# One written order for TensorE, ScalarE and VectorE in the units of a state space layer

## The chip, the core and the metric

The kernel runs on one core of a Trainium2 chip, as one launch. The core has five engines with a queue each: TensorE (PE: matrix products and transposes), VectorE (DVE), ScalarE (ACT), GpSimd (POOL) and SyncE (SP, which issues most of the DMAs).[...] The metric is the device time of a launch in microseconds (us), and the kernel before stands at a median of 3936.15 us over three runs (3933.37 to 3936.95).

## The reference

The model is a decoder of four layers on 2048 tokens (16 sequences of 128) with 256 features; each layer has a self-mixing part, a cross attention and a feed-forward part. The change is in the self-mixing part of layer 2, a bidirectional state space layer. Per direction it computes:

```python
zxbcdt = x @ in_w.T                         # z: 512, xBC: 768, dt: 8 heads
dt = jax.nn.softplus(zxbcdt[..., D_INNER + CONV_CH:] + dt_bias)
conv = sum((xp[:, k:k + l, :] * conv_w[:, k] for k in range(D_CONV))) + conv_b
xBC = silu(conv)                            # -> xs (512), B (128), C (128)
L = jnp.exp(segsum(Adt))
Y_diag = jnp.einsum('bcln,bcsn,bhcls,bcshp->bclhp', Cc, Bc, L, X)
y = ssd(xh, dt, A, B, C) + xh * D[None, None, :, None]
y = rmsnorm(y * silu(z), gnorm_w)
return y @ out_w.T
```

`x` is normalised over its features first, and the outputs of the two directions go through a common output matrix and are added to the residual. A sequence is one chunk of 128, so only `Y_diag` is left of the scan.

## The kernel before, in words

The program is written with a layer that schedules: the text issues instructions in some order, and a scheduler sets each engine's final order by priorities and by its own estimates, except where an instruction is marked `keep_in_program_order`. Marked instructions keep the written order among themselves on their engine. In the kernel before only the products and transposes of this layer are marked (`pinned`, L253, and `pinned_transpose`, L258; the profile gives all of them line 255 or 258, so tiles tell them apart). ACT and DVE are ordered by the scheduler.

`l2_attn` works on four groups `g` of four sequences (512 tokens in a group) and two directions `f` and `b`: 8 units, `m` from 0 to 7, with `g, i = divmod(m, 2)`. Each unit has these steps:

- `channels`: six channel blocks `ch` (0 to 3 are xs, 4 is B, 5 is C). For each: a 128x512 product `xBC` on PE (L1191), the convolution's first tap with its bias on ACT (L1194), its other three taps on DVE (L1199, `scalar_tensor_tensor` on PSUM), and `Silu` in place on ACT (L1202).
- `gates`: four products `z` (L1209) and their Silu (L1210).
- `sums`: cumulative sums of the decays by four small products `cs`, then `left` and `cs` on DVE (L1219, L1221) and `right` on POOL (L1223).
- For each half `n` of the heads: `decays` (eight products `seg` into two double PSUM tiles, then two `Exp` on ACT that give `w`, L1253); `products` for n = 0 (`cb`, copied by ACT, L1263); `by_token` (eight transposes `xtok`, then `xd` on DVE with the factor dt, L1275); `weigh` (`w` times `cb` on DVE, L1285); `outputs` (products `y`, then on DVE the `D` term, L1304, and the gate, L1305).
- `squares` (ACT, L1311), `lengths` (products `ss`, a copy `ssb` on DVE, a transpose `sst`, `Sqrt` on ACT, reciprocal on DVE) and `project` (four times four products `proj`, each added to x with the row's factor on DVE, L1334).

The units overlap by the order of the text in the loop at L1386: while unit m goes through its two halves, unit m+1's channels (4, 5, 0 in the first half; 1, 2, 3 in the second) and gates and unit m-1's lengths and projection are written between them.

PSUM limits how far an engine may run ahead: `b1` has four buffers of 128x512, which every one of `xBC`, `z`, `cs`, `cb`, `xtok`, `y`, `ss`, `sst`, `proj` and `pw` takes in turn, and `b2` has two double buffers, taken by `seg`. A product waits until the last reader of its buffer's former tile is through. ACT has to load a table of functions when it changes between Exp, Silu, Sqrt and Ln; the loads are instructions of their own in its queue.

Ahead of the units stand the normalisation of the four groups (L1156 to L1177: statistics, `rstd`, `ss`, the scaling of `h`, eight transposes `tr` per group and their copies to `hT`), unit 0's channels and gates, the products `dt` over all groups and the softplus chain on DVE and ACT (L1343 to L1377), and 16 products `pw` that merge the two output matrices (L1383, L1384).

Of the kernel before, what the change touches and what calls it, by code (L numbers as in the profile page):

```python
# [16 lines left out]
P = 128  # L17
# [12 lines left out]
class Decoder:  # L30
# [1076 lines left out]
    def l2_attn(self):  # L1107
# [15 lines left out]
        with self.tc.tile_pool(name="l2a", bufs=1) as wk:  # L1123
# [32 lines left out]
            for g in range(NG):  # L1156
# [21 lines left out]
            def start(m):  # L1178
                return dict(
                    xs=wk.tile([P, 6, GT], F, tag="xs", name="xs", bufs=2), z=wk.tile([P, 4, GT], F, tag="z", name="z", bufs=2)  # L1180
                )

            def channels(m, u, chs):

                g, i = divmod(m, 2)
                d = dirs[i]
                cw, cbias = self.c(f"L2_{d}_conv_w"), self.c(f"L2_{d}_conv_b")
                for ch in chs:
                    ps = self.b1("xBC")
                    for k in range(2):  # L1190
                        self.pinned(ps, wx[d][:, k, ch * P : (ch + 1) * P], hTs[g][:, k, :], start=k == 0, stop=k == 1)  # L1191
                    x = u["xs"][:, ch, :]
                    w = lambda k: cw[:, ch * 4 + k : ch * 4 + k + 1]
                    nc.scalar.activation(x, ps, AF.Identity, scale=w(3), bias=cbias[:, ch : ch + 1])  # L1194
                    x3, p3 = (v.rearrange("p (t n) -> p t n", t=GB) for v in (x, ps))
                    for n in range(1, 4):
                        late, early = slice(n, P), slice(0, P - n)
                        dst, src = (late, early) if d == "f" else (early, late)
                        nc.vector.scalar_tensor_tensor(  # L1199
                            x3[:, :, dst], p3[:, :, src], w(3 - n), x3[:, :, dst], ALU.mult, ALU.add  # L1200
                        )
                    nc.scalar.activation(x, x, AF.Silu)  # L1202

            def gates(m, u):
                g, i = divmod(m, 2)
                for c in range(4):
                    ps = self.b1("z")
                    for k in range(2):
                        self.pinned(ps, wz[dirs[i]][:, k, S(c)], hTs[g][:, k, :], start=k == 0, stop=k == 1)  # L1209
                    nc.scalar.activation(u["z"][:, c, :], ps, AF.Silu)  # L1210

            def sums(m, u):

                g, i = divmod(m, 2)
                ps = self.b1("cs")[:, 0:P]
                for t in range(GB):
                    self.pinned(ps[R(t), :], da[:, i, g * GB + t, :], upto[dirs[i]], start=True, stop=True)
                left = wk.tile([P, P], F, tag="left", name="left", bufs=2)
                nc.vector.tensor_scalar(left, ps, kind[:, 1:2], kind[:, 0:1], ALU.mult, ALU.add)  # L1219
                cs = wk.tile([P, P], F, tag="cs", name="cs", bufs=2)  # L1220
                nc.vector.tensor_scalar(cs, ps, kind[:, 0:1], kind[:, 1:2], ALU.mult, ALU.add)  # L1221
                right = wk.tile([P, NH, P], F, tag="right", name="right", bufs=1)
                nc.gpsimd.tensor_tensor(  # L1223
                    right,
                    cs.unsqueeze(1).to_broadcast([P, NH, P]),
                    each.unsqueeze(2).to_broadcast([P, NH, P]),
                    ALU.mult,
                )
                u["left"], u["right"] = left, right

            def decays(m, u, n):

                tiles = [self.b2("seg").rearrange("p (t n) -> p t n", t=2) for _ in range(2)]
                for t in range(GB):
# [3 lines left out]
                        never[dirs[m % 2]].unsqueeze(1).to_broadcast([P, 4, P]),  # L1238
# [3 lines left out]
                for t in range(GB):  # L1242
                    self.pinned(
                        tiles[t // 2][:, t % 2, :],
                        u["left"][R(t), :],
                        u["right"][R(t), 4 * n : 4 * n + 4, :].rearrange("p h l -> p (h l)"),
                        start=False,
                        stop=True,
                    )
                ws = []  # L1250
                for ps in tiles:
                    w = wk.tile([P, 2, 4, P], F, tag="w", name="w", bufs=2)
                    nc.scalar.activation(w.rearrange("p t h l -> p t (h l)"), ps, AF.Exp)  # L1253
# [3 lines left out]
            def products(m, u):  # L1257

                ps = self.b1("cb")
                for t in range(GB):  # L1260
                    self.pinned(ps[:, S(t)], u["xs"][:, 4, S(t)], u["xs"][:, 5, S(t)], start=True, stop=True)
                cb = wk.tile([P, GB, P], F, tag="cbm", name="cbm", bufs=2)
                nc.scalar.copy(cb.rearrange("p t n -> p (t n)"), ps)  # L1263
                u["cb"] = cb

            def by_token(m, u, n):

                g, i = divmod(m, 2)
                xd = self.hp.tile([P, GB, 4, 64], F, tag="h", name="xd", bufs=2)
                for t0 in (0, 2):  # L1270
                    ps = self.b1("xtok").rearrange("p (t c n) -> p t c n", t=2, c=2)
                    for t in range(2):
                        for c in range(2):
                            self.pinned_transpose(ps[:, t, c, :], u["xs"][:, 2 * n + c, S(t0 + t)])
                    nc.vector.tensor_tensor(  # L1275
                        xd[:, t0 : t0 + 2],
                        ps.rearrange("p t c (h d) -> p t (c h) d", h=2),
                        dt[:, i, g * GB + t0 : g * GB + t0 + 2, 4 * n : 4 * n + 4].unsqueeze(3).to_broadcast([P, 2, 4, 64]),
                        ALU.mult,
                    )  # L1280
                return xd

            def weigh(u, ws):
                for i, w in enumerate(ws):
                    nc.vector.tensor_tensor(  # L1285
                        w, w, u["cb"][:, 2 * i : 2 * i + 2, :].unsqueeze(2).to_broadcast([P, 2, 4, P]), ALU.mult
                    )

            def outputs(m, u, n, ws, xd):

                D = self.c(f"L2_{dirs[m % 2]}_D")
                for c in range(2):
# [10 lines left out]
                    x, z = u["xs"][:, 2 * n + c, :], u["z"][:, 2 * n + c, :]  # L1303
                    nc.vector.scalar_tensor_tensor(x, x, D[:, 2 * n + c : 2 * n + c + 1], ps, ALU.mult, ALU.add)  # L1304
                    nc.vector.tensor_tensor(z, x, z, ALU.mult)  # L1305
# [3 lines left out]
            def squares(m, u):  # L1309
                for c in range(4):  # L1310
                    nc.scalar.activation(sq[:, c, :], u["z"][:, c, :], AF.Square)  # L1311

            def lengths(m, u):

                ps = self.b1("ss")[:, 0:P]
                for c in range(4):
                    for t in range(GB):
                        self.pinned(ps[R(t), :], self.ones[:, 0:32], sq[:, c, S(t)], start=c == 0, stop=c == 3)
                s = wk.tile([P, P], F, tag="ssb", name="ssb", bufs=1)
                nc.vector.tensor_copy(s, ps)  # L1320
                ps = self.b1("sst")[:, 0:P]
                self.pinned_transpose(ps, s)
                rs = self.small([P, GB], "yss")
                self.rsqrt(rs, ps.rearrange("p (t n) -> p t n", t=GB)[:, :, 0], 1.0 / 512)
                u["rs"] = rs

            def project(m, u):
                g, i = divmod(m, 2)
                for t in range(GB):
# [688 lines left out]
```

## Time and profile before

| | us |
|---|---|
| median of three runs | 3936.15 |
| the profiled execution: device time | 3932.67 |
| its span, first to last instruction | 3931.0 |
| PE busy | 3587.0 (91%) |
| DVE busy | 2106.7 (54%) |
| ACT busy | 1441.8 (37%) |
| POOL busy | 490.4 (12%) |
| mean granted TensorE clock | 0.938 of full |
| stretch of the state space layer in the span | about 1809 to 2197 |

A matrix product in fp32 shows as two records, and the ends of PE's records are modelled, so a busy PE is not PE at its peak; the distance between the starts of two groups tells more. A bracket behind a row of the timeline gives the idle time of that engine before it and what ended it. A wait for several semaphores is put down to the one that came last. "PEclk" is the share of the full clock that TensorE was granted.

### The profile page before, as it was taken

Reading aid. Unit: us, or ns where it says so; the run is one execution under the profiler, and the core shown is the slowest. Engines: PE = TensorE matmul, PEld = TensorE weight load, DVE = VectorE, ACT = ScalarE, POOL = GpSimd, SP = SyncE. Lnnn points to the kernel's source line nnn. Section 1 sums busy time; section 2 is a strip of 40 time slices with the busy share of each in tenths; the row PEclk is TensorE's granted clock in tenths of the full one; section 3 lists DMA queues with packets and bytes.
Section 4 is the critical chain, followed back from the end, with each engine's and each line's share of the span. In section 5 each row is a group of like instructions: output and inputs, shape, how many; then the busy total and the mean of one; then the engine's idle time right before and its main releaser. Section 6 shows DMA issues by size and latency. Waiting matters only on the chain.

```text
span 3931.0 us, 52987 instructions
## 1 busy us (share of the span) xinstructions
PE 3587.0 (91%) x22096; PEld 1919.0 (49%) x22096; DVE 2106.7 (54%) x4165; ACT 1441.8 (37%) x1893; POOL 490.4 (12%) x620
## 2 busy tenths in 40 slices
PE   7988999999998899967898995679999999999999
PEld 4655555555556566634455564442222222223665
DVE  5436344444544444465666445247777777772440
ACT  2334111111134322255655221112666666664221
POOL 5322000000013211152000200120000000001100
PEclk9977799999999999988999996887999999999989
DMA  3000000000110100000000000820000000000000
GB/s 91 9 1 5 9 17 20 20 21 18 35 34 2 35 1 1 20 25 13 1 1 11 2 1 31 284 75 0 1 1 1 1 6 12 17 1 13 1 8 17
DMA packets 73638, 84.65 MB, mean 22 GB/s; under 512 B 5587, under 2 KB 61206, under 8 KB 73142
## 3 DMA queue, kind: packets, MB, share of 16 engines
q1 hardware_dynamic: 65510, 71.04, 5.8%
q10 hardware_dynamic: 6352, 6.03, 0.5%
q0 software_dynamic: 1536, 4.20, 0.3%
q8 instruction: 174, 2.85, 0.3%
q14 instruction: 66, 0.54, 0.0%
HBM read 71.02 MB, written 10.22 MB: 21 GB/s over the span
## 4 chain that ended last, share of the span: by engine, by line
PE 81%; DVE 10%; POOL 3%; ACT 3%; issue 2%; DMA 1%; POOLq 0%; ACTq 0%; DVEq 0%
PE st L1728 9%; PE acc L1728 6%; PE down L166 6%; PE gate L166 6%; PE up L166 6%; PE proj L255 5%; PE smax L1728 4%; PE st L255 4%; PE qT L166 3%; PE o L255 2%; PE h L255 2%; PE rb L255 2%; DVE mx L1776 2%; PE v L886 1%; PE kT L886 1%
## 5 line engine op out<-in xcount | busy, mean ns | idle before, releaser
L1776 DVE TENSOR_REDUCE mx<-smax 128x1 f32<-128x512 f32 x1024 | 635.0, 683 | 178.2 <-PE smax L1728 178.2
L1831 ACT ACTIVATE e<-st 128x1024 f32<-128x1024 f32 x512 | 521.4, 1023 | 351.9 <-PE st L1728 332.5
L1728 PE MATMUL st<-qT,kT 32*128 32x512 f32 x2048 | 569.0, 646 | 3.4 <-ACT e L1831 3.4
L649 DVE SCALAR_TENSOR_TENSOR x<-down,w_all,x 128x256 f32<-128x256 f32 x512 | 212.2, 477 | 315.3 <-PE down L166 315.3
L638 ACT ACTIVATE gs<-gate,cols 128x512 f32<-128x512 f32 x132 | 90.7, 687 | 583.8 <-PE gate L166 583.7
L1728 PE MATMUL smax<-kb,qb 32*128 32x512 bf16 x1024 | 274.1, 395 | 7.7 <-DVE mx L1776 5.4
L1728 PE MATMUL acc<-e,v 128*32 128x512 f32 x2048 | 274.4, 608 | 0.2 <-ACT e L1831 0.2
L166 PE MATMUL gate<-hT,expert 128*128 128x512 f32 x528 | 250.0, 596 | 0.0
L166 PE MATMUL down<-expert,gs 128*128 128x256 f32 x1056 | 249.4, 379 | 0.5 <-DVE gs L639 0.5
L166 PE MATMUL up<-hT,expert 128*128 128x512 f32 x528 | 248.7, 593 | 0.0
L166 PEld LDWEIGHTS down<-expert,gs 128*128 128x128 f32 x1056 | 200.6, 190 | 84.0 <-DVE gs L639 31.7
L1728 PEld LDWEIGHTS st<-qT,kT 32*128 32x128 f32 x2048 | 153.4, 184 | 154.6 <-issue 117.1
L1728 PEld LDWEIGHTS <-qb 32*128 32x128 bf16 x1024 | 54.3, 93 | 290.4 <-issue 276.8
L166 PEld LDWEIGHTS gate<-hT,expert 128*128 128x128 f32 x528 | 100.7, 191 | 126.6 <-issue 126.3
L166 PEld LDWEIGHTS up<-hT,expert 128*128 128x128 f32 x528 | 100.8, 191 | 72.1 <-issue 65.4
L988 DVE TENSOR_TENSOR cT<-o,rb 128x512 f32<-128x512 f32 x64 | 44.3, 692 | 164.6 <-ACT rb L986 164.6
L1728 PEld LDWEIGHTS acc<-e,v 128*32 128x32 f32 x2048 | 40.4, 108 | 187.0 <-issue 185.9
L986 ACT COPY rb<-rb 128x512 f32<-128x512 f32 x64 | 37.5, 585 | 252.4 <-PE rb L255 252.4
L166 PE MATMUL qT<-hT,L_xattn_Wq 128*128 128x512 f32 x256 | 115.8, 606 | 8.2 <-issue 4.3
L183 PE MATMUL tr<-ident,h 128*128 128x128 f32 x352 | 63.4, 327 | 58.5 <-DVE h L205 33.5
L255 PE MATMUL o<-e,v 128*32 128x128 f32 (+1 forms) x2048 | 105.9, 281 | 11.8 <-DVE nm L292 11.8
L639 DVE SCALAR_TENSOR_TENSOR gs<-up,cols,gs 128x512 f32<-128x512 f32 x132 | 99.0, 751 | 24.4 <-PE up L166 8.1
(512 smaller groups left out, 5725.3 us busy)
## 6 DMA issues: line engine op xcount, KB each, us to landing
W<-in_L_ffn_W_dram SPq DMA_DIRECT2D x46, 512.0 KB, 4.4
expert<-in_L_ffn_Wg_dram SPq DMA_DIRECT2D x32, 128.0 KB, 2.1
expert<-in_L_ffn_Wu_dram SPq DMA_DIRECT2D x32, 128.0 KB, 2.2
expert<-in_L_ffn_Wd_dram SPq DMA_DIRECT2D x32, 128.0 KB, 2.4
hs<-zero SPq DMA_DIRECT2D x23, 128.0 KB, 1.9
ys<-yo ACTq DMA_DIRECT2D x23, 128.0 KB, 3.9
hb<-hs ACTq DMA_DIRECT2D x5, 512.0 KB, 3.9
x<-in_x_dram SPq DMA_DIRECT2D x4, 512.0 KB
```

Source lines behind the costliest of these rows:

```text
L166: self.nc.tensor.matmul(out, lhsT, rhs, start=i == 0, stop=i == n - 1 and bias is None)
L183: self.nc.tensor.transpose(ps[:, t * P : (t + 1) * P], src[:, t, k * P : (k + 1) * P], self.ident)
L255: self.tc.keep_in_program_order(self.nc.tensor.matmul(*a, **k))
L638: nc.scalar.activation(gs, pg, AF.Silu, bias=bg)
L639: nc.vector.scalar_tensor_tensor(gs, pu, bu, gs, ALU.add, ALU.mult)
L649: nc.vector.scalar_tensor_tensor(xt, pd[:, t, :], w_all[:, o : o + 1], xt, ALU.mult, ALU.add)
L886: nc.tensor.matmul(ps, l, r, start=True, stop=False)
L986: nc.scalar.copy(rb, ps)
L988: nc.vector.tensor_tensor(cT, po, rb, ALU.mult)
L1728: self.tc.keep_in_program_order(nc.tensor.matmul(*a, **k))
L1776: nc.vector.tensor_reduce(mx[:, kc, j : j + 1], ps, AX.X, ALU.max)
L1831: nc.scalar.activation(e[:, 2 * jj : 2 * jj + 2, :], ps, AF.Exp, scale=1.0 / 16.0)
```

## The change

Nothing of what is computed changes, and the products keep their shapes. It has three parts.

First, the steps are taken apart so that the text can place each engine's share on its own: `channel` and `silu` of one block, `gate` of one block, `weigh` and `gated` apart from `by_token` and `outputs`, `project` and `add` of one sequence, and `sums` and `length` as generators that stop between their parts. `squares` is done by halves.

Second, ACT's and DVE's instructions of the units are marked to keep their written order too (`act`, `copy`, `tt`, `ts`, `stt`), as PE's already were.

Third, the written order is new, in the loop and ahead of it. Unit 0's channels and gates follow group 0's normalisation, ahead of the other three groups'; `sums` of unit 0 stands ahead of `pw`.

```diff
-            for g in range(NG):
+            def tokens(g):
                 ...
+            pin = self.tc.keep_in_program_order
+            act = lambda *a, **k: pin(nc.scalar.activation(*a, **k))
+            copy = lambda *a: pin(nc.scalar.copy(*a))
+            tt = lambda *a: pin(nc.vector.tensor_tensor(*a))
+            ts = lambda *a: pin(nc.vector.tensor_scalar(*a))
+            stt = lambda *a: pin(nc.vector.scalar_tensor_tensor(*a))
...
+            def weigh(u, n, ws, tiles):
+                ...
+                by_cb(0)
+                by_dt(0)
+                by_dt(1)
+                by_cb(1)
+                return xd
...
+            def length(u):
+                ps = self.b1("ss")
+                for c in range(4):
+                    for t in range(GB):
+                        self.pinned(ps[R(t), 0:P], self.ones[:, 0:32], sq[:, c, S(t)], start=c == 0, stop=c == 3)
+                s = wk.tile([P, P], F, tag="ssb", name="ssb", bufs=1)
+                pin(nc.vector.tensor_copy(s, ps[:, 0:P]))
+                yield
+                self.pinned_transpose(ps[:, P : 2 * P], s)
+                u.rs = self.small([P, GB], "yss")
+                act(u.rs, ..., AF.Sqrt, bias=self.eps[:, 0:1], scale=1.0 / 512)
+                pin(nc.vector.reciprocal(u.rs, u.rs))
+                yield
...
-            us = {0: start(0)}
-            channels(0, us[0], (4, 5, 0, 1, 2, 3))
-            gates(0, us[0])
+            tokens(0)
+            u = Unit(0)
+            for ch in (4, 5, 0, 1, 2, 3):
+                channel(u, ch)
+                silu(u, ch)
+            for c in range(4):
+                gate(u, c)
+            for g in range(1, NG):
+                tokens(g)
...
+            for _ in sums(u):
+                pass
             (16 products pw)
-            sums(0, us[0])
             for m in range(M):
-                (two halves: decays, products, by_token, weigh, next unit's
-                 channels, outputs, last unit's lengths and project, gates)
+                after = Unit(m + 1) if m + 1 < M else None
+                ws = decays(u, 0)
+                if last:
+                    gated(last, 1, ys)
+                products(u)
+                xt = by_token(u, 0)
+                if last:
+                    squares(last, 1)
+                xd = weigh(u, 0, ws, xt)
+                if after:
+                    channel(after, 4)
+                    channel(after, 5)
+                if last:
+                    mean = length(last)
+                    next(mean)
+                    if after:
+                        channel(after, 0)
+                    po = [project(last, t) for t in range(2)]
+                    next(mean)
+                    for t in range(2):
+                        add(last, t, po[t])
+                elif after:
+                    channel(after, 0)
+                ys = outputs(u, 0, ws, xd)
+                gated(u, 0, ys)
+                if last:
+                    for t in range(2, GB):
+                        add(last, t, project(last, t))
+                    if not last.i:
+                        (bias added to this group's x on POOL)
+                squares(u, 0)
+
+                ws = decays(u, 1)
+                xt = by_token(u, 1)
+                if after:
+                    cs = sums(after)
+                    next(cs)
+                xd = weigh(u, 1, ws, xt)
+                if after:
+                    next(cs)
+                    channel(after, 1); gate(after, 0); silu(after, 4)
+                    channel(after, 2); gate(after, 1); silu(after, 5)
+                    channel(after, 3); silu(after, 0); gate(after, 2)
+                    silu(after, 1); silu(after, 2); gate(after, 3); silu(after, 3)
+                ys = outputs(u, 1, ws, xd)
+                last, u = u, after
+            gated(last, 1, ys); squares(last, 1)
+            po = [project(last, t) for t in range(2)]
+            mean = length(last)
+            next(mean); next(mean)
+            for t in range(GB):
+                add(last, t, po[t] if t < 2 else project(last, t))
```

## The prediction

> **What bounds the kernel now.** I began with the page: TensorE (PE) is busy 91% of the span, so the state space layer counts by what TensorE loses in it. The stretches of the layer, in the view of busy time by window (columns: window, its length, busy us and instructions of PE, weight loads, DVE, ACT, POOL, then the granted clock):
>
> ```profile
> 1809.00:1856.00 47.00, 35.55 (x136) 19.53 (x135) 29.94 (x65) 25.73 (x41) 0.48 (x3) 0.88 0.03 7
> 1856.00:1896.00 40.00, 34.65 (x160) 17.88 (x160) 25.31 (x36) 22.30 (x28) 3.79 (x2) 0.83 0.06 23
> 1896.00:2156.50 260.50, 232.90 (x1355) 134.14 (x1352) 169.57 (x281) 152.75 (x195) 18.43 (x9) 0.97 0.02 5
> 2156.50:2197.00 40.50, 32.44 (x243) 24.45 (x243) 24.39 (x45) 13.68 (x17) 2.39 (x2) 0.87 0.00 1
> ```
>
> They are the opening, unit 0, units 1 to 6 and unit 7 with the end: 388 us. Units 1 to 6 take 43.4 us each, with DVE at 65% and ACT at 59%: no engine is full, so it is waits that cost. One unit runs from the `seg` group at 2026.82 to the next at 2068.94; in its timeline these are the largest stalls of PE (start, us, engine, line; in brackets the idle time before and who ended it):
>
> ```profile
> 2033.37 3.70 PE L255 MATMUL xBC<-hT,L_b_wx 128*128 128x512 f32 x8 [0.76 <-ACT cbm L1263]
> ...
> 2040.55 1.08 PE L255 MATMUL ss<-squares,ones 128*32 128x128 f32 x32 [0.86 <-ACT xs L1202]
> ...
> 2043.87 0.33 PE L258 MATMUL sst<-ident,ssb 128*128 128x128 f32 x1 [2.24 <-DVE ssb L1320]
> ```
>
> Ends are modelled, so I count PE by starts of one group to the next: two `seg` groups of 2.04, `cb` 0.89, two `xtok` 0.88, six channels 1.71, four gates 1.72, two `y` groups 1.90, four `proj` 1.69, `ss`, `cs`, `sst` 1.35 together: 35.8 us at full clock. The unit took 42.1. The largest hole (2.24) is `sst`, behind a DVE queue full of convolutions.
>
> The clock is the second loss. After the holes of the opening it halves:
>
> ```profile
> 1858.00:1860.00 2.00, 1.18 (x8) 0.51 (x8) 0.00 (x0) 0.00 (x0) 0.77 (x1) 0.50 0.19 67
> 1860.00:1862.00 2.00, 2.00 (x13) 1.16 (x6) 0.00 (x0) 1.05 (x2) 0.00 (x0) 0.50 0.00 0
> 1862.00:1864.00 2.00, 2.00 (x12) 2.00 (x11) 0.19 (x1) 1.47 (x2) 0.00 (x0) 0.50 0.04 8
> 1864.00:1866.00 2.00, 2.00 (x7) 1.28 (x7) 1.84 (x3) 0.00 (x0) 0.00 (x0) 0.84 0.00 0
> 1866.00:1868.00 2.00, 2.00 (x6) 0.80 (x6) 2.00 (x3) 0.78 (x1) 0.00 (x0) 1.00 0.00 0
> ```
>
> PE is busy again from 1858.83, and the clock is back only by about 1865.3.
>
> **The change part by part.** The built program shows that DVE and ACT stand in the written order, and no engine's order changes outside this layer.
>
> *Units 1 to 6.* I laid one unit out by hand from those starts, each instruction at the later of its queue's turn and its inputs (plus 0.3 us from PE to ACT or DVE, 0.05 between the others, as the timeline shows), with four `b1` buffers. DVE, start to start: convolution step 0.65, `w` 1.2, `xd` 0.65, four gated steps 2.86, `proj` add 0.45. ACT: `Exp` pair 1.94, copy 0.5, channel 0.75, `Silu` 0.6, square 0.6, table load 1.28. From the start of `seg` (0):
>
> - First half. Exponentials 2.15 to 4.1, `cb` copy to 4.6; DVE `w`, `xd` twice, `w` to 8.3, then channels 4 and 5 to 10.3 and 12.3, `ssb` 12.6, channel 0 to 14.6. PE: `cb`, `xtok`, channels 4 and 5 to 7.24 without a wait, `ss` 8.1, channel 0 to 9.8. First `proj` needs channel 4's buffer: 10.4 (0.6 lost); second needs channel 5's: 12.4 (0.3); then `sst` at 14.1, no longer waiting for `ssb`. `y` needs channel 0's buffer and the root: 14.7 (0.5). Two `proj`, and the second half starts at 20.0.
> - Second half. The squares must end (19.4) and the Exp table load (20.7) before the exponentials at 22.15: just hidden. `w` to 24.35, so PE goes on with `cs` and channel 1; the gate at 25.0 finds its buffer. Channels and gates alternate to 35.25 with 0.1 us waits; `y` ends at 37.15.
>
> So 37.15, of which 1.4 is wait. The other edits of a unit cost nothing of their own: the instructions are the same in number, and `sst` now lies in `ss`'s tile, one `b1` tile fewer, but held from 7.2 to the root at 14.7, which is in the wait of `y`. In units 2, 4 and 6 the next layer's `rstd` stands in ACT's queue before the exponentials; it needs the last two adds and their statistics (22.0), so rstd ends 22.35, load 23.6, exponentials 1.45 late; `w` and `xd` follow and the first gate waits 1.5 us: 38.7. Sum 3 × 37.15 + 3 × 38.7 = 227.6; I add 0.25 a unit for latencies not seen: 229. Before: 260.4. Gain 31.
>
> [...] I expect full clock. The trace of before has a granted clock of 0.91 in several 20 us windows here; each dip is a few us at half rate and lies in the 43.4.
>
> *ACT's table loads.* A unit loses one Silu load (exp, sqrt, exp, silu are left: 4 instead of 5 or, with rstd, 7):
>
> ```profile
> L1253 ACT ACT_TABLE_LOAD x17 | 21.8, 1283 | 0.9 <-PE seg L255 0.6
> ...
> L1202 ACT ACT_TABLE_LOAD x15 | 19.2, 1283 | 11.1 <-DVE xs L1199 11.1
> ```
>
> By the built programs 50 in the layer become 36: 14 × 1.28 = 18 us of ACT, which hides beside PE, so nothing in the sum. The row is 1.28 us, and at 2029.61 the next exponential follows its load by 0.01 us. [...] I take the row.
>
> *The opening.* Channels and gates of unit 0 now follow the first 8 transposes on PE, at about 1811.8 instead of 1824.4. But each ACT `Silu` stands before the next channel's ACT step, so a channel is a serial chain: ACT 0.78, three DVE steps 2.05, Silu 0.62, in all 3.5 us against 1.71 on PE. ACT also changes table four times round group 3's rstd and ss. By hand: channel 4 is through at 20.3 (+1800), 5 at 24.5, then four of 3.5 to 38.5; the last gate needs channel 3's buffer (37.9), so PE has it done at 39.7. Behind it in PE's queue are 24 transposes; group 3's normalisation stands behind all convolutions on DVE (h 44.5, x 45.7), ACT scales to 47.4, transposes and copies to 48.4. `dt` starts at 1848.4; before it was 1843.7: 4.6 us later. No DMA moves: SP's queue has the same order. On POOL the four bias adds stand one place earlier; each (2.35 us) runs from 20.8 in a unit, and the next `right` is not due before 27.5.
>
> *The fill behind dt.* The 16 `pw` products used to run in the hole of the softplus chain:
>
> ```profile
> 1843.72 1.94 PE L255 MATMUL dt<-hT,wdt 128*32 128x512 f32 x16
> ...
> 1846.89 7.09 PE L166 MATMUL pw<-L_wbT,out_w 128*128 128x256 f32 x32
> ...
> 1855.57 0.43 PE L255 MATMUL cs<-tri_up,da 128*32 128x128 f32 x8 [1.59 <-DVE da L1377]
> ...
> 1858.83 2.09 PE L255 MATMUL seg<-right,left 32*128 32x512 f32 x8 [1.86 <-POOL right L1223]
> ```
>
> Now `cs` stands before `pw`. From dt to cs takes 11.0 (11.8, less 0.8 of DVE steps that pw's evictions had delayed); then cs 0.4, pw 6.75, seg 2.04. The hole of 8 us halves the clock. [...] The trace shows some 6 us (1858.83 to 1865.3), so 3.0 lost. Dt to `cb` is then 23.2[...] against 17.1. With the later dt, `cb` comes 10.7 late.
>
> *Unit 0* has no proj or ss. Laid out likewise 33.2 us from `cb` to `cb`; its squares hold back the second exponentials until 17.6. Before: 37.2, with half a clock at both ends. Gain 4.0; unit 1 starts 6.7 late.
>
> *Unit 7 and the end*: 40.3 from seg to the last proj before. By hand 33.7, plus 2 for a clock halved by a 3.9 us wait for `w`: 35.8. Gain 4.5.
>
> Sum: +6.7 - 31.3 - 4.5 = -29. The profiled execution had a span of 3931.0 in 3932.7 us; it becomes 3902 and 3904. The median of the runs is 3.5 above it: 3936.15 - 29 = 3907. Bounds: latencies 0 to 1.5 us a unit more or less (9), opening 0 to 14 late instead of 10.7, end ±3.
>
> **The rivals.**
> - The full gain: units at PE's floor, 6 × 35.8 = 215, gain 46, and the opening no worse than before: with 4 and 4.5, 3882. For it: PE is the fullest engine. Against: the serial channels. 12 in 100.
> - Half the gain: DVE's strict queue puts 41 us on a unit, as its steps' own records (conv 0.74, w 1.26) are longer than their starts apart, and every proj waits. Gain 14, less 6.7, plus 4.5: 3924. 16 in 100.
> - Slower: in the ACT queue the squares of the first half stand before the exponentials of the second. If the gated product is late, exponentials, `w`, `xd` and the gates' buffers all slip and the PE clock halves. My slack there is 0.1 us, so every us late is a us of the unit; from 4.8 us a unit the change loses (29 / 6), and at 7 it gives 3949. For it: squares in before waited up to 8.2 us for DVE's z. Against: z is due at 18.7, and 3 us would already take another fault upstream. 7 in 100.
> - No effect, gains and opening cancelling: 3936. 4 in 100.
> - The forecast: 61 in 100.
>
> **How the numbers follow.** A measurement of this kernel can tell 0.2% (8 us) from no change. The forecast's own range is 3894 to 3920. Below lies the full gain; above, half the gain mostly. From 3887 to 3927 leaves out about 2 in 10. Faster (below 3928): forecast 0.61, full gain 0.12, most of half the gain 0.15, so 0.88. Within: 0.04 and 0.01 of half the gain. Slower (above 3944): 0.07.
>
> **What would show it.** Unit starts 37.4 us apart (39.0 with rstd); `sst` without a wait; a clock of 1.0 throughout units 1 to 6; `dt` near 1848, `pw` after `cs` at half clock; 36 table loads. Wrong if unit starts stay over 41 us apart, or exponentials of the second half start over 2 us after their seg.

## The result, and the profile after

The changed kernel takes 3909.95 us (median of five runs, 3909.65 to 3916.67), the kernel before 3936.15 (3927.30 to 3938.74). The ratio is 0.9941, 95% interval 0.9927 to 0.9956: 0.6% faster. The forecast was 3907.

Total times are a coarse ruler here. In the thirteen profiled executions of this study the layer's first transposes behind the last `down` start between 1803.80 and 1813.64 us, although every edit lies inside the layer. So I compare the layer by itself: from the transposes `tr` behind the last `down` of the layer ahead to the first `kT` of the cross attention that follows. Before: 1809.49 to 2196.60, 387.1 us. After: 1807.21 to 2174.28, 367.1 us. The layer gained 20.0 us; of the profiled execution's gain (3932.67 to 3909.95, 22.7) the other 2.7 lie outside it.

Busy time by stretch in the changed kernel (stretch, its length, busy us and instructions of PE, weight loads, DVE, ACT, POOL, then granted clock, DMA share and GB/s):

```profile
1807.00:1858.00 51.00, 31.96 (x94) 13.48 (x93) 28.01 (x57) 28.46 (x43) 0.48 (x3) 0.80 0.02 3
1858.00:1902.60 44.60, 40.52 (x201) 23.08 (x202) 28.84 (x44) 17.55 (x25) 3.79 (x2) 0.91 0.08 25
1902.60:2138.90 236.30, 226.32 (x1353) 129.91 (x1352) 175.65 (x280) 133.57 (x184) 18.44 (x9) 1.00 0.02 5
2138.90:2174.30 35.40, 30.50 (x243) 22.93 (x243) 21.68 (x40) 12.82 (x17) 2.35 (x1) 0.90 0.00 1
```

The third line is units 1 to 6: 236.3 us where they took 260.5, PE busy for 96% of it, and the clock at 1.00 instead of 0.97. The first two, opening and unit 0, got longer: `dt` starts 38.1 us after the first transposes (34.2 before), `cb` of unit 0 at 62.3 (51.4), unit 1 at 95.3 (86.6).

| | forecast | measured |
|---|---|---|
| `dt` of the opening | 4.6 later | 3.9 later |
| `dt` to `cb` | 23.2 | 24.2 |
| unit 1's start | 6.7 later | 8.8 later |
| units 1 to 6 | 229 (37.4 and 39.0 a unit, in turn) | 236.2 (39.37 every unit) |
| unit 7 and the end | 35.8 | 35.4 |
| the layer | 29 shorter | 20.0 shorter |

The same unit's timeline of PE as shown of before, now from 2020.67 (start, us, engine, line):

```profile
2024.58 3.60 PE L255 MATMUL xBC<-hT,L_b_wx 128*128 128x512 f32 x8
2028.11 1.08 PE L255 MATMUL ss<-squares,ones 128*32 128x128 f32 x32
...
2035.18 0.27 PE L258 MATMUL ss<-ident,ssb 128*128 128x128 f32 x1
...
2047.65 1.98 PE L255 MATMUL z<-hT,L_b_wz 128*128 128x512 f32 x4 [1.02 <-DVE xd L1185]
```

The three waits shown of before (0.76, 0.86, 2.24 us) carry no bracket any more. The largest wait left in the first half is 0.33 us. One new wait of a microsecond stands in the second half: the first gate, behind `xd`. The chain of the next unit's second half, whose `seg` starts at 2080.78, says where that comes from (the chain counts a group from where the one before it ends; the parts of a unit that are compared with the forecast below are measured by it):

```profile
2080.78 2.00 PE seg L255 x12
2082.78 0.01 issue
2082.79 0.08 ACT L1183
2082.87 1.21 issue
2084.09 1.03 ACT w L1183
2085.12 0.02 issue
2085.14 1.22 DVE w L1185
2086.36 0.61 DVE xd L1185
2086.98 0.04 issue
2087.02 1.98 PE z L255 x4
```

An ACT instruction without a tile name (0.08, then 1.21 counted as issue) stands between `seg` and the exponentials. ACT's own timeline names it:

```profile
2082.79 1.28 ACT L1183 ACT_TABLE_LOAD   x1 [2.97 <-PE seg L255]
2084.09 1.94 ACT L1183 ACTIVATE w<-seg 128x1024 f32<-128x1024 f32 x2
```

ACT was free for 2.97 us and loaded the Exp table only when `seg` was done. The layer holds 36 table loads, as forecast; here one of them is open in full.

The opening. Behind `dt` PE stands for 7.41 us, and then works at half clock (granted clock 0.50 from 1853 to 1862):

```profile
1845.30 3.95 PE L255 MATMUL dt<-hT,wdt 128*32 128x512 f32 x16
1849.93 0.66 PE L258 MATMUL dtt<-ident,dT 128*128 128x128 f32 x4 [0.68 <-ACT dT L1387]
1858.00 0.66 PE L255 MATMUL cs<-tri_up,da 128*32 128x128 f32 x8 [7.41 <-DVE da L1416]
1858.58 9.02 PE L166 MATMUL pw<-L_wbT,out_w 128*128 128x256 f32 x32
```

`pw` takes 9.02 us where it took 7.09, and `dt` itself 3.95 where it took 1.94 (granted clock 0.50 from 1846 to 1848; 1.00 under the `dt` of before).

### The profile page after: what moved, and what is told of

The parts are those of the page before. It is cut to its first block, busy times and chain, and to the rows that moved or that the text cites. A ratio compares the mean times of both kernels' runs of the same rounds, so it can differ in the third digit from the quotient of the medians.

```text
span 3908.2 us, 52952 instructions
## 1 busy us (share of the span) xinstructions
PE 3579.1 (92%) x22096; PEld 1911.3 (49%) x22096; DVE 2112.2 (54%) x4165; ACT 1419.5 (36%) x1879; POOL 490.8 (13%) x620
## 3 DMA queue, kind: packets, MB, share of 16 engines
q8 instruction: 174, 2.85, 0.3%
## 4 chain that ended last, share of the span: by engine, by line
PE 80%; DVE 10%; ACT 3%; POOL 3%; issue 2%; DMA 1%; SPq 0%; POOLq 0%; ACTq 0%; DVEq 0%
PE st L1805 9%; PE acc L1805 6%; PE down L166 6%; PE gate L166 6%; PE up L166 6%; PE proj L255 5%; PE smax L1805 4%; PE st L255 4%; PE qT L166 3%; PE o L255 2%; PE h L255 2%; PE rb L255 2%; DVE mx L1853 2%; PE v L886 1%; PE kT L886 1%
## 5 line engine op out<-in xcount | busy, mean ns | idle before, releaser
L1187 DVE SCALAR_TENSOR_TENSOR xs<-xBC,cols,xs 128x508 f32<-128x508 f32 x144 | 106.1, 741 | 22.2 <-ACT xs L1183 18.8
```

Source lines behind the costliest of these rows:

```text
L1187: stt = lambda *a: pin(nc.vector.scalar_tensor_tensor(*a))
```

## The experiments

My theory after the result: the units gained what the forecast says less one open table load and some tenths, and the opening lost in two separate places, the chain of Silus and the clock behind `dt`. The rival: the gain is ACT's and DVE's fixed order as such, or one cause lies behind both losses of the opening. Each run below is a variant of the changed kernel unless it says otherwise, and the layer's length is what is compared (changed kernel 367.1).

**A table load brought forward.** A one-element exponential behind the squares makes ACT load the table while it has nothing to do.

```diff
                 squares(u, 0)
+                act(pre, self.eps[:, 0:1], AF.Exp)
 
                 ws = decays(u, 1)
```

> A one-element Exp on ACT behind the first half's squares, so that the Exp table is loaded before the second half's exponentials are due. Theory (the load of 1.28 us waits for seg together with the exponential and so lies open in each unit): units 38.1 us apart instead of 39.37, the layer from the transposes behind the last down product to the first kT 358 us instead of 367.2. Rival (the exponentials are late because squares and rstd stand before them in ACT's queue): 39.4, as the new instruction stands behind the same squares.

Measured: 3909.59 us, layer 366.5. Units 1, 3 and 5 take 38.09 us, but units 2 and 4 now take 40.0 and unit 6 takes 42.0. ACT's timeline of unit 4 of this run:

```profile
2035.67 1.28 ACT L1183 ACT_TABLE_LOAD   x1
2036.96 0.20 ACT L1183 ACTIVATE pre<-eps 128x1 f32<-128x1 f32 x1
2037.18 1.28 ACT L191 ACT_TABLE_LOAD   x1
2038.48 0.30 ACT L191 ACTIVATE rstd<-bnmv,eps 128x4 f32<-128x4 f32 x1
2038.80 1.28 ACT L1183 ACT_TABLE_LOAD   x1
2040.09 1.94 ACT L1183 ACTIVATE w<-seg 128x1024 f32<-128x1024 f32 x2
```

The next layer's `rstd`, which nothing holds in place, fell between the early exponential and the real ones: a Sqrt table and a second Exp table in a row. In unit 6 PE stood 1.96 us ahead of the first gate, 1.64 in units 2 and 4, and there that gate took 3.47 us where it took 1.98 in units 2 and 4. The gain of the odd units was given back in the even ones. So the early exponential was left out there:

```diff
                 squares(u, 0)
+                if not (last and last.i):
+                    act(pre, self.eps[:, 0:1], AF.Exp)
```

> The one-element exponential of the run before is now left out in the units whose ACT queue also holds the next layer's rstd (2, 4 and 6), where it only added two table loads. Theory (the Exp table load stands with seg's wait and is open by its own 1.28 us in the second half of every unit without rstd): units 1, 3 and 5 take 38.1 us, 2, 4 and 6 stay at 39.4; also unit 0 and unit 7 gain up to 1.3 each; the layer from its first transposes to kT takes 367.2 - 3 x 1.28 - 0 to 2.6 = 361 to 363. Rival (the load is not what is open; the 38.1 of the run before came from something else the early instruction moved): units 1, 3 and 5 stay at 39.4, layer 367.

Measured: layer 362.9 (3916.18 us, with the layer beginning at 1813.64). Unit starts at 1909.17, 1947.27, 1986.64, 2024.74, 2064.11, 2102.21, 2141.59: 38.10 and 39.37 in turn. The layer gained 4.2: three times 1.28, and 0.4 in the other stretches. In each odd unit just the load's duration disappears, so it was the load that was open.

Why does it wait for `seg` at all? The built program's ACT queue in the second half of such a unit says (the run with the early exponential below the changed kernel):

```
changed kernel, unit 1:     Activation squares    waits DVE
                            LoadActFuncSet        waits PE
                            Activation w<-seg     waits Activation
with the early exponential: LoadActFuncSet
                            Activation pre<-eps
                            Activation w<-seg     waits PE, Activation
```

In this build the exponential has two semaphores to wait for, and the first of the two sits on the load right ahead of it. The kernel before has exponentials with one wait in units 1 to 6, and the loads ahead of them do not wait (in unit 1 the load starts at 1915.02, 1.03 us of waiting for `seg` follow it, and the exponentials start at 1917.33). The other two traces agree: in the changed kernel the load starts at 2082.79, when `seg` ends; with the early exponential, in unit 5, it starts at 2083.82, straight behind the squares, and the exponentials only at 2086.81, behind `seg`.

**The sums behind `pw`.** The first unit's `sums` moved behind the 16 `pw` products, where the kernel before had them.

```diff
-            for _ in sums(u):
-                pass
-
             pw = wk.tile([P, 2, 4, DM], F, tag="pw", name="pw")
...
+            for _ in sums(u):
+                pass
             M = 2 * NG
```

> Only unit 0's cumulative sums are put back behind the 16 pw products. Theory (pw lay in the hole of the softplus chain, and now stands open behind it): from dt to cb 17 us instead of 24.2, the layer 361 us instead of 367.2. Rival (the hole halves the clock anyway, and the seg group then pays it): 20 us, the layer 364.

Measured: 3905.00 us, layer 360.3, 6.8 shorter. PE's timeline:

```profile
1843.34 4.00 PE L255 MATMUL dt<-hT,wdt 128*32 128x512 f32 x16
1848.51 7.09 PE L166 MATMUL pw<-L_wbT,out_w 128*128 128x256 f32 x32
1857.18 0.42 PE L255 MATMUL cs<-tri_up,da 128*32 128x128 f32 x8 [1.59 <-DVE da L1416]
1860.44 2.09 PE L255 MATMUL seg<-right,left 32*128 32x512 f32 x8 [1.86 <-POOL right L1233]
1862.46 1.84 PE L255 MATMUL cb<-xs 128*128 128x128 f32 x8
```

`pw` at 7.09 fills the hole again and `dt` to `cb` is 19.1 in place of 24.2; another 1.7 came in unit 0. (It is not the expected 17 because `dt` still takes 4.00 where it took 1.94 before; at half clock in the changed kernel it took 3.95.) Two short waits are left (1.59, 1.86), and the clock halves once more there (0.50 from 1861 to 1863, `seg` 2.09), only later.

**Each Silu one channel later** in unit 0:

```diff
+            prev = None
             for ch in (4, 5, 0, 1, 2, 3):
                 channel(u, ch)
-                silu(u, ch)
+                if prev is not None:
+                    silu(u, prev)
+                prev = ch
+            silu(u, prev)
```

> In unit 0 each Silu stands one channel later in the text, so that ACT takes the next channel's first tap before it waits for this channel's convolution. Theory (ACT step, convolution and Silu in series make 3.72 us a channel): about 2.3 us a channel, dt 31 us after the transposes behind the last down product instead of 38.1, the layer 361 us. Rival (the table loads for group 3's roots and the 24 transposes behind the gates set it): dt at 36 or later, the layer 365 or more.

Measured: 3912.29 us, but the layer began at 1813.05; it takes 360.1, 6.9 shorter, with `dt` 30.5 after the first transposes. In the changed kernel ACT waits in every channel for the convolution, Silu to Silu 3.72 us:

```profile
1825.65 0.63 ACT L1183 ACTIVATE xs<-xs 128x512 f32<-128x512 f32 x1 [2.42 <-DVE xs L1187]
1826.18 0.76 ACT L1183 ACTIVATE xs<-xBC,cols 128x512 f32<-128x512 f32 x1
1829.37 0.63 ACT L1183 ACTIVATE xs<-xs 128x512 f32<-128x512 f32 x1 [2.43 <-DVE xs L1187]
```

The chain of the forecast was there, and one place in ACT's queue removes it.

**All rows ahead of the first unit's channels**, the order of before for this part:

```diff
-            tokens(0)
+            for g in range(NG):
+                tokens(g)
             u = Unit(0)
...
-            for g in range(1, NG):
-                tokens(g)
```

> All four groups are normalised before unit 0's channels, as before; all else as in the changed kernel. Theory (the series of Silu and channel costs, not the place): the chain starts 13 us later and nothing follows it, dt at 41 instead of 38.1, the layer 370 us. Rival (the place ahead of the other rows made dt late): dt at 34 as before, the layer 363.

Measured: 3916.64 us, layer 370.4; `dt` 43.2 after the first transposes instead of 38.1. With the serial chain in place, starting it early is worth 3.3 us of the layer.

**Nothing held on ACT and DVE.** The new text and PE's order stay; ACT and DVE are the scheduler's again (the planner of the expectation).

```diff
-            pin = self.tc.keep_in_program_order
+            pin = lambda i: i
```

> The changed kernel with its written order kept only on PE; on ACT and DVE the order is chosen by the planner again, as in the kernel before. In the built program the planner swaps only neighbours there: the order inside the pairs xd and w, Silu and the next channel, and the squares of unit 0 between its two exponentials. Theory (the new sequence of groups, above all on PE, and not the pinning of ACT and DVE is what gained): units of 39 to 41 us, opening up to 7 us shorter because Silus move behind the next channel's first step, layer 355 to 372. Rival (the pins on ACT and DVE are what gained): units back at 43.4 us and more, layer over 387.

Measured: 3899.05 us, layer 354.7, 12.4 shorter than the changed kernel. Units take 39.74 us, 0.37 longer. `dt` starts at 29.6 (38.1), unit 0 takes 30.4 from `seg` to `seg` (35.1). So in this run holding ACT and DVE to the text gains 2 us in units 1 to 6 and costs 14.5 ahead of them, and what the units gained over the kernel before comes for the most part (3.7 of 4.0 us a unit) from the new sequence of groups. In this build the exponentials of the second half carry one wait and the second half takes 17.4 us (18.7 in the changed kernel); the first half, in which a unit has five table loads where the changed kernel has one, takes 22.3 (20.7). That the loads cost this time is not shown.

**The order of before, held.** The kernel before, with ACT and DVE held to its own text (every `nc.scalar` and `nc.vector` call of the units):

```diff
+            pin = self.tc.keep_in_program_order
+            pinned_scalar_activation = lambda *a, **k: pin(nc.scalar.activation(*a, **k))
...
-                    nc.scalar.activation(x, x, AF.Silu)
+                    pinned_scalar_activation(x, x, AF.Silu)
```

> The kernel before, with its own sequence of groups and with the opening as before, but ACT and DVE held to the order in which its text names the operations. Theory (pins gain nothing by themselves; in that text each Silu stands right behind its channel's three steps and three channels follow one another in a half, a chain of 3.7 us a channel): units of 44 to 50 us, layer 392 to 440, slower than before. Rival (being held to a written order is itself the gain, because the planner's order was bad): units under 42 us, layer under 380.

Measured: 4003.56 us, layer 456.9: further out than I expected, units of 52.3 to 54.4 us. ACT in one of them:

```profile
2026.62 0.63 ACT L1179 ACTIVATE xs<-xs 128x512 f32<-128x512 f32 x1
2027.15 0.76 ACT L1179 ACTIVATE xs<-xBC,cols 128x512 f32<-128x512 f32 x1
2030.34 0.63 ACT L1179 ACTIVATE xs<-xs 128x512 f32<-128x512 f32 x1 [2.42 <-DVE xs L1183]
```

It is the opening's chain of 3.72 us a channel, now three times in every half. A fixed order is worth what the text puts into it; by itself it is no gain.

**The transpose of the lengths back in its old place**, straight behind `ss`:

```diff
                     next(mean)
+                    next(mean)
                     if after:
                         channel(after, 0)
                     po = [project(last, t) for t in range(2)]
-                    next(mean)
```

> The changed kernel with the transpose of the squared lengths put back to its old place, straight behind ss on PE: ahead of channel 0 and of the first two proj instead of behind them. Theory (on DVE ssb stands behind the six steps of channels 4 and 5, so it is done 12.7 us after the unit's start while PE reaches the transpose at about 8.5; PE waits some 4 us, partly given back because the first proj needs channel 4's buffer until 10.5 anyway): 2 to 4.5 us on a unit, units of 41.4 to 43.9, the layer at 381 to 394. Rival (the transpose's place costs nothing, the units' gain comes from the other orders): units stay at 39.4, layer 367.

Measured: 3942.68 us, layer 400.7, units of 44.2 to 45.0: more than either expectation. PE's timeline:

```profile
2042.65 1.08 PE L255 MATMUL ss<-squares,ones 128*32 128x128 f32 x32
2048.03 0.33 PE L258 MATMUL ss<-ident,ssb 128*128 128x128 f32 x1 [4.30 <-DVE ssb L1347]
2048.20 3.00 PE L255 MATMUL xBC<-hT,L_b_wx 128*128 128x512 f32 x4
2050.98 4.24 PE L255 MATMUL proj<-pw,z 128*128 128x256 f32 x16
```

PE waits 4.30 us for `ssb`, and channel 0, which started straight behind `ss` in the changed kernel (2029.12, 1.01 us after it), stands behind the transpose in PE's queue and waits with it. Then the clock is at half for 3.4 us (2048.8 to 2052.2, granted clock 0.50 in 2049 to 2052): channel 0 takes 3.00 instead of 1.98. The hole and its clock together cost 4.8 to 5.6 us a unit. With the other orders as they are, this one place in PE's queue is worth more than the units' whole gain over the kernel before (4.0 us a unit). Whether moving the transpose alone would have gained anything in the kernel before, where it waits 2.24 us, was not run.

**Taps of channels 4 and 5 in turn** on DVE:

```diff
-                    channel(after, 4)
-                    channel(after, 5)
+                    pair(after, 4, 5)
...
```

> The changed kernel, with the three steps of channels 4 and 5 of the next unit alternating on DVE (first tap of 4, first of 5, second of 4 ...) in place of one channel after the other. Theory (a convolution step that follows a step on the same tile starts 0.74 us behind it, one that follows a step on another tile 0.65): the six steps take 3.9 us in place of 4.4; channel 4's buffer comes free 1.5 us later, the first proj of the last unit with it, so a unit gains or loses at most 0.5 us. Rival (the 0.74 us is the step's own duration whatever precedes it): six steps 4.4 us still, and a unit about 1 us longer for the later buffer.

Measured: 3910.08 us, layer 365.4. Six steps in the changed kernel, in this run, and in the kernel before:

```profile
2028.73 4.50 DVE L1187 SCALAR_TENSOR_TENSOR xs<-xBC,cols,xs 128x508 f32<-128x508 f32 x6
```

```profile
1990.00 3.98 DVE L1187 SCALAR_TENSOR_TENSOR xs<-xBC,cols,xs 128x508 f32<-128x508 f32 x6
```

```profile
2051.99 3.99 DVE L1199 SCALAR_TENSOR_TENSOR xs<-xBC,cols,xs 128x508 f32<-128x508 f32 x6 [0.20 <-ACT xs L1194]
```

Four of the six steps no longer follow a step on their own tile, and 0.52 us are gone: such a step starts 0.78 us behind the one on its tile and 0.65 behind another, 0.13 more (not the 0.09 of the expectation). The units still became 0.17 us longer (39.54): PE now waits 1.12 us for DVE ahead of the first `proj`, whose buffer is channel 4's. The layer is shorter by 1.6 because unit 0 is 2.2 shorter, and its order differs by these six steps only: the clock in 1890 to 1895 was 1.00 here and 0.69 in the changed kernel.

**Three edits together**: the early exponential where it is free, the sums behind `pw`, the Silus one channel later (diffs as above).

> Three edits of the changed kernel in one: the early one-element exponential in the units without rstd, the first sums behind pw, and in unit 0 each Silu one channel later. Theory (they act in three different places: the open table load, the clock lost behind dt, the serial chain of unit 0): the gains of the single runs add, 4.2 + 6.8 + 7.0 = 18.0 us; the layer takes 349 us, and the time is 0.9855 to 0.991 of the kernel before, some 3897. Rival (they share one cause: an opening without the long hole keeps the clock, so that one of the opening's edits alone gives both gains): layer 353 to 357.

Measured: 3897.13 us (3890.50 to 3898.81; the kernel before stood at 3929.47 beside it), ratio to before 0.9911, interval 0.9897 to 0.9925; layer 349.0. The layer is 18.1 shorter, and the single gains add to 17.9. Each edit gives its gain in its own stretch: `dt` is 7.55 us earlier (the Silus alone: 7.55), `dt` to `cb` 5.2 shorter (`pw` alone: 5.05), units 1 to 6 3.8 shorter (the early exponential alone: 3.8). So the two losses of the opening and the open load are three causes. That the totals agree so closely is luck in part: unit 0 took 35.4 us from `cb` to `cb`, where it took 33.4 with `pw` moved alone (here the first gate took 3.68 us behind a hole of 2.27 us; in units 1 to 6 of the changed kernel, at a clock of 1.00, it takes 1.98), and the end was 1.3 shorter than with the early exponential alone.

**ACT and DVE held from unit 1 on**, with the early exponential and the sums behind `pw`:

```diff
-            pin = self.tc.keep_in_program_order
+            held = []
+            pin = lambda i: self.tc.keep_in_program_order(i) if held else i
...
+                if m == 1:
+                    held.append(True)
                 after = Unit(m + 1) if m + 1 < M else None
```

> The changed kernel with ACT and DVE held to the written order from unit 1 on only (opening and unit 0 are left to the planner there), plus the early one-element exponential in units without rstd and the first sums behind pw. Theory (in the opening and in unit 0 holding to the text costs 9.8 and 4.1 us beside the run with nothing held on ACT and DVE; from unit 1 on it gains nothing or little): dt 29.6 us after the layer's first transposes, seg of unit 0 at about 47, unit 1 28.5 to 30.3 us after it, units 38.1 and 39.4 in turn, the layer at 343 to 346, the time 0.984 to 0.990 of the kernel before. Rival (the opening's gain in that run came from the first unit's later steps, which are held again here): layer 352 or more.

Measured: 3890.28 us (3882.62 to 3893.28), ratio 0.9891, interval 0.9875 to 0.9908; layer 345.8. By its median this is the fastest version of the study. Its interval overlaps that of the run above; its layer is 3.2 shorter. `dt` came at 32.5, not 29.6; the section at the end shows where the 2.9 us lie. Unit 1 started 33.4 us behind unit 0, not 28.5 to 30.3: PE waits 1.86 us for `right` in the middle of `seg`, and the clock is at half from 1857.6 to 1861.0 (granted clock 0.50 in 1858 to 1861).

## Why the prediction was right or wrong

**Direction and size.** Faster was right, and the total came out 2.95 us from the forecast. That closeness is partly luck: the layer gained 20.0 us where the steps say 29. The profiled executions differ by 2.7 us outside the layer, and the before median lies another 3.5 above its profiled execution.

**Units 1 to 6: the term that was mis-sized.** Forecast 229, gain 31; measured 236.2, gain 24.1. The mechanism held: `sst` and channels without waits, clock at 1.00 throughout. By the parts of the layout (forecast, measured, from the unit's start): second half begins 20.0, 20.67; its exponentials stand 2.15 behind their `seg`, 3.31; the first gate 2.85 behind the exponentials, 2.93; from that gate to the unit's end 12.15, 12.47. The difference of 2.2 us is thus half the table load. The step that failed reads "the squares must end (19.4) and the Exp table load (20.7) before the exponentials at 22.15: just hidden". The squares did end in time, but the load carried `seg`'s wait and could not use the free ACT ahead of it; the layout had the loads in the queue and not what they wait for. The rest is tenths: six convolution steps take 4.4 us (`ssb` follows at 2033.15), not 4.0, because the layout's 0.65 a step had been read in the trace of before and held order puts steps on one tile behind each other; and the last two `proj` of the first half take 3.65, not 3.4. Of the signs named for being wrong one showed: counted from the start of `seg` the exponentials came 3.31 us behind it, over the 2 us named. The layout itself had 2.15 there, so the sign had been set too tight; from the end of `seg` it is 1.31.

**The units with `rstd`** did not take 1.55 us more: 39.37 like the others. Only because the others had their load open as well; once it is closed there (38.10), `rstd` costs 1.27 in comparison (its own load, too, still starts with the end of `seg`, 0.21 us after ACT is free). The forecast's difference was right in kind, hidden by the fault above.

**Table loads.** 36 in the layer, as forecast. For their price I took the row of 1.28 us in the profile of before. The open loads measure 1.28, exponential 0.01 us behind (2082.79 to 2084.09), and closing one gains 1.28: the row was the right choice.

**The opening.** `dt` 3.9 late (4.6), `cb` 10.9 late (10.7). The serial chain of Silus is confirmed by moving it (6.9 us; a channel took 3.72 where the layout had 3.5), `pw` out of its hole by moving it back (6.8). Inside `dt` to `cb` two terms cancelled: `dt` ran at half clock, 2.0 us that I had not counted, and behind the hole the clock was back 4.4 us after PE started (1858.0 to 1862.4), not 6, which gives 0.8 back: 23.2 + 2.0 - 0.8 = 24.4, measured 24.2. I had taken my 6 us as a constant. It isn't one: behind three other holes of this trace the clock was back 10.9, 5.0 and 4.6 us after PE started again (the last section has them). (In the trace of before, too, the clock was back sooner than the forecast read: a mean of 0.84 from 1864 to 1866 puts it at 1864.6, not 1865.3.)

**Unit 0** took 35.1 us from `cb` to `cb`, forecast 33.2, with a clock of 0.69 for 5 us that the layout had at 1. The run with the taps in turn has the same hole of 2.17 us ahead of its first gate, but a clock of 1.00 there, and took 32.9. That fits the clock as the main term that was missing (3.4 us at half, 1.7 lost), but no run changed the clock alone.

**Unit 7 and the end**: 35.4, forecast 35.8.

**The rivals.** The full gain fell with the opening and the open load. Half the gain asked for 41 us a unit: its argument (step records longer than starts apart) was true of the convolution and worth tenths. The slower rival, squares ahead of late exponentials, did not occur; `sst` in its old place shows that the loss it speaks of, 4.8 us a unit, was one wrong place away.

## What to carry to other kernels

A written order for an engine is worth what stands in it: look in it for pairs that wait for each other back to back (a Silu right behind the convolution that feeds it), because the scheduler had moved them here, and a fixed order repeats the chain in every pass (here 3.72 us a channel). Hold an engine only where its order has been laid out: here holding ACT and DVE gained 0.37 us a unit in the loop and cost 14.5 us ahead of it. Where a table load stands ahead of an activation, look at what the load itself waits for; here an early one-element activation of the same function took its 1.28 us off the path in three units, and cost 0.6 to 2.6 us in the three where an activation of another table fell between. Compare the stretch that the edit touches by its own first and last group, not by the total, when other parts of the program vary by more than the edit is worth.

## What the runs showed of the hardware

**Behind which hole the clock fell.** Between 1820 and 1870 the granted clock changed in the changed kernel in these windows of one microsecond (the clock is the third number from the end; all windows between the first pair, the second and the third are at 0.50):

```profile
1821.00:1822.00 1.00, 1.00 (x3) 0.33 (x2) 0.00 (x0) 0.99 (x2) 0.00 (x0) 0.70 0.00 0
1831.00:1832.00 1.00, 1.00 (x3) 0.34 (x1) 0.96 (x2) 0.00 (x0) 0.00 (x0) 0.68 0.00 0
1845.00:1846.00 1.00, 1.00 (x5) 0.34 (x8) 0.69 (x1) 0.59 (x1) 0.00 (x0) 0.65 0.00 0
1848.00:1849.00 1.00, 1.00 (x8) 0.00 (x0) 0.00 (x0) 0.00 (x0) 0.00 (x0) 0.65 0.00 0
1852.00:1853.00 1.00, 0.00 (x0) 0.00 (x0) 0.00 (x0) 0.99 (x2) 0.00 (x0) 0.56 0.00 0
1862.00:1863.00 1.00, 1.00 (x5) 0.83 (x5) 0.48 (x1) 0.00 (x0) 0.00 (x0) 0.82 0.00 0
```

A mean of 0.70 over a microsecond that ends at half means 0.6 us at half, so the clock fell at 1821.40; the other times follow likewise. Beside the longest holes of PE in the opening and unit 0 of this trace:

| hole of PE ahead of | us | PE starts again | granted clock |
|---|---|---|---|
| `xBC` of channel 3 | 2.48 | 1820.70 | half from 1821.4 to 1831.6 |
| the last gate | 1.77 | 1836.87 | 1.00 from 1832 to 1845 |
| the last `tr` | 3.16 | 1843.74 | half from 1845.3 to 1848.7 |
| `cs` | 7.41 | 1858.00 | half from 1852.1 to 1862.4 |
| unit 0's first gate | 2.17 | 1888.45 | half from 1889.7 to 1893.1 |

In three of the four falls PE was busy again when the clock fell, 0.7 to 1.6 us after the hole's end; in the long hole it fell 1.5 us after the hole had begun. `dt`, at half for 3.4 us, took 3.95 where it took 1.94 before. How long the clock stays down differs too, 3.4 to 10.2 us here (a second hole, of 1.89 us, lies in the first stretch).

**The same hole, two prices.** With nothing held in the opening, PE stands 2.98 us ahead of the gates in two runs with the same order there (but for a one-element exponential in ACT's free time). In the first (nothing held at all):

```profile
1826.03 7.11 PE L255 MATMUL z<-hT,L_f_wz 128*128 128x512 f32 x16 [2.98 <-issue]
```

and in the second (held from unit 1 on):

```profile
1824.42 10.04 PE L255 MATMUL z<-hT,L_f_wz 128*128 128x512 f32 x16 [2.98 <-issue]
```

The clock stays at 1.00 from 1820 to 1832 in the first and is at half from 1823.5 to 1830.3 in the second. The 2.9 us between the gates of the two runs are the whole difference of their `dt`. The kernel before shows it within one trace: units 1 to 6 all have the same 2.24 us ahead of `sst`, and the clock stayed at 1.00 around it in units 2 and 4 (1957 to 1966 and 2043 to 2051) and fell to 0.50 in the other four (in 1914 to 1919, 2002 to 2004, 2087 to 2089 and 2131 to 2134).

Standing time alone did not decide in these runs. The first of these lines is from the changed kernel, the hole of 1.77 us behind which the clock stayed at 1.00; the others are from the run with the sums behind `pw`, two holes of 1.44 us together, and there the four records of `xBC` took 3.53 us where they took 1.98 in unit 0 of the changed kernel (at 1884.30, clock 1.00):

```profile
1836.87 1.95 PE L255 MATMUL z<-hT,L_f_wz 128*128 128x512 f32 x4 [1.77 <-DVE xs L1187]
```

```profile
1875.33 0.63 PE L258 MATMUL xtok<-ident,xs 128*128 128x128 f32 x4 [0.48 <-DVE xs L1187]
...
1877.27 3.53 PE L255 MATMUL xBC<-hT,L_b_wx 128*128 128x512 f32 x4 [0.96 <-DVE xs L1187]
```

What else decides was not shown. For the reader of a profile it means that part of a few microseconds' difference between two builds can be a hole that both have and that lowered the clock in one of them only, and not the edit (2.9 us above).
